# One fused graph, attention and expert layer: graph work placed earlier, two tiles turned later, expert choice from one partition

## The chip, the core and the metric

The kernel runs on one core of a Trainium2 chip. The metric is the device time of one execution in microseconds, the median of repeated runs on the chip. The core has TensorE (PE, with its weight loads PEld), VectorE (DVE), ScalarE (ACT), GpSimd (POOL) and SyncE (SP), which here only issues transfers. Each engine takes its instructions in order, so an instruction that waits holds all that stand behind it on that engine. The granted clock is the share of TensorE's full clock that the profiler records.

## The reference

The layer has 1250 tokens of width 768, all in float32. A graph with 21250 edges (`src`, `dst`) is fixed by the inputs. Cut to what matters:

```python
xn = layernorm(x)
# graph branch: two attention layers over the edges, with 4 and 2 heads
out1 = gat(layernorm(xn), edges, W1, 4 heads)
out2 = gat(out1, edges, W2, 2 heads)
graph = concat([xn, out2]) @ Wu + bu
# mixing branch: linear attention, then an MLP 768 -> 3072 -> 768
m = xn + linear_attention(layernorm(xn))
mix = m + gelu(layernorm(m) @ fc1 + fc1_b) @ fc2 + fc2_b
x = x + graph + mix
# experts: one choice of 2 of 4 for the whole sequence
v = layernorm(x)
logits = v.mean(tokens) @ router_w.T + router_b
e1, e2 = top2(logits);  g1, g2 = softmax of the two logits
out = x + layernorm(g1 * expert[e1](v) + g2 * expert[e2](v) + v)
```

An expert is 768 -> 1536 -> 768 with its own activation (gelu, silu or mish). Which expert's weights are needed is known only after the mean over all tokens.

## The kernel before

**Stages.** Tokens are held as 10 tiles of 125, or, turned, as `fT` (features on partitions). Matrices are multiplied with Strassen-like seven products: `differences` and `by_tokens` form the token-side differences in four VectorE operations per chunk of tokens, `combined` the weight-side ones. The stages follow each other: weight folding and the `Wu` product, the first graph product (`ps_g`), keys and values, queries and projection, the MLP with the graph attention woven into it, the choice of experts, then the two experts (`unit`, `second`) and the last tiles.

**Edges to a table.** The 21250 edges become a dense 1250 x 1250 table of counts in DRAM. `edge_piece` and `later_pieces` work through 10 pieces of 17 columns. For each piece a row of keys is broadcast to all partitions (`kr`, `load_keys`, 1062.5 KB), VectorE compares it with a column of keys and counts repeats (L295, L300, L305), and GpSimd issues 17 indirect transfers that add counts to one of two tables in turn (L315, 170 in all). `edge_piece(i)` of the first four pieces asks for the keys of piece i + 2 as soon as the buffer of piece i is free; before the change GpSimd's queue issues that load. When all 170 are done, `merged` adds the second table to the first by block of 125 rows (L1115), and `fetch` reads a block back (L1128).

**The graph in the MLP.** `gnn()` is a Python generator. Its first part, `largest`, finds the largest score per token: it issues three `merged`, then two `fetch`, yields, and then per block makes a mask `far` on VectorE (L1143) and updates a running maximum for each head (L1151 for the first block, L1147 for the others). Each `yield` carries a price in microseconds of TensorE time. The MLP loop pays with `spend`: 2.04 or 1.36 for one of the seven products of fc1, 1.39 for one half tile of fc2. The first call of `next(steps)` comes when the credit reaches zero:

```python
steps = gnn()
credit, cost = -44.0, 0.0
def spend(us):
    nonlocal credit, cost
    credit += 1.05 * us
    while cost is not None and credit >= cost:
        credit -= cost
        cost = next(steps, None)
```

The MLP takes 12 groups `g`, each with a chunk `c` of 4 token tiles and one of 6 (`MIX_TILES`); the patterns of `P` (an fc1 product) and `h` (a half tile of fc2, L1077, evicted by L1082 on VectorE) give the order of emission. `pin` keeps an instruction in order of the program among pinned ones of its engine; the framework's planner orders the rest by its own estimate of when operands are ready.

**The end of the MLP.** After the last half of a tile, `last_tile` calls `normal` (statistics, and the normalised tile `y`), and two tiles later `turned`: six matrix products against an identity with one more column of ones, which give `fT` and, in the last column, the sum over tokens (`pooled`). Of tile 9 the sum comes from seven other products (`ps_s9`, L1420 and L1425), so that it needn't wait for `y`.

**The choice.** `ps_g` (L1468) multiplies the sum with the router's weights, with the sum broadcast so that all 128 partitions get the 4 logits. `choose` finds the first expert in seven VectorE operations, and its number goes through a register of SyncE (`values_load`) into the address of the weights (`load_first`, L1545). Meanwhile TensorE turns tile 9 (L1479), then `warm(13)` multiplies identities.

**The experts.** For each pair `q` of hidden blocks and chunk `c`, `unit` makes seven products in two halves. `tables` has ScalarE work out four activation functions of the unit before, and `blended` mixes them on VectorE (L1530 to L1532).

Of the kernel before, what the change touches and what calls it, by code (L numbers as in the profile page):

```python
# [8 lines left out]
F32 = mybir.dt.float32  # L9
BF16 = mybir.dt.bfloat16  # L10
I32 = mybir.dt.int32
# [12 lines left out]
MIX, MIX_TILES = [(0, 250), (250, 375)], [(0, 1, 5, 6), (2, 3, 4, 7, 8, 9)]  # L24
# [8 lines left out]
def tile_gps_layer(ctx, tc, a, out):  # L33
    nc = tc.nc
# [66 lines left out]
    def differences(engine, of, to, c0, w):  # L101
        x11, x12, x21, x22 = (x[:, :, c0 : c0 + w] for x in of)
        t1, t2, t4 = (to[:, i, :, c0 : c0 + w] for i in range(3))
        for o, p, q in ((t1, x12, x11), (t2, x22, t1), (x12, x22, x12), (t4, x21, t2)):
            engine.tensor_tensor(o, p, q, ALU.subtract)

    def by_tokens(engine, to, c0, w):
        of = (fT[:, 0:3, :HALF], x12, fT[:, 3:6, :HALF], fT[:, 3:6, HALF:])
        differences(engine, of, to, c0, w)
# [212 lines left out]
    def edge_piece(i):  # L322
        kr = keys.pop(i)
        if i + 2 < SOON:
            load_keys(i + 2, nc.gpsimd)
        for _ in edge_steps(i, ep, kr, ((PIECE,),) * 3):
            pass
# [1036 lines left out]
    credit, cost = -44.0, 0.0  # L1364

    def spend(us):
        nonlocal credit, cost
        credit += 1.05 * us
        while cost is not None and credit >= cost:
            credit -= cost  # L1370
            cost = next(steps, None)

    ready = []

    def last_tile(t):
        normal(t)
        ready.append(t)
        if len(ready) > 2:
            turned(ready.pop(0))
# [14 lines left out]
    for g in range(GROUPS):  # L1394
# [4 lines left out]
        for c, pattern in enumerate(("PPhhhhPhhPPhhPPhhhh", "PPhhPhhPPhhPPhh")):  # L1399
            if g == GROUPS - 1 and c:  # L1400
# [3 lines left out]
                gnn_pool.__exit__(None, None, None)  # L1404
            parts = fc1_unit(g, c)
# [8 lines left out]
    for x in todo:  # L1414
        put_half(*x)
    turned(ready[0])

    t9 = NT - 1
    ps = bank("ps_s9")
    pin(nc.tensor.matmul(  # L1420
        ps[:, :KC], r3[:, t9, 1:2].to_broadcast([TP, 128]),
        identx[:, TP:].to_broadcast([TP, KC]), start=True, stop=False, skip_group_check=True,
# [42 lines left out]
    sels = const.tile([128, 2, 4], F32, name="sels")  # L1465
    ps = bank("ps_g")
# [8 lines left out]
    for j in range(2):  # L1475
        ps = bank4("ps_t")
        for i in range(3):
            k = 3 * j + i
            pin(nc.tensor.transpose(  # L1479
                ps[:, i, :TP], y[:, t9, k * 128 : (k + 1) * 128], ident[:TP, :TP]  # L1480
            ))
        nc.scalar.copy(fT[:, 3 * j : 3 * j + 3, t9 * TP :], ps[:, :3, :TP])
    warm(13)
    es = []

    def choose(j):
        l, m, first = lg[:, j, :], top[:, j, 0:1], top[:, j, 1:2]
        pin(nc.vector.tensor_reduce(m, l, AX.X, ALU.max))
        at = const.tile([128, 4], F32, name=f"at{j}")
        pin(nc.vector.scalar_tensor_tensor(at, l, m, order, op0=ALU.is_equal, op1=ALU.mult))  # L1490
        pin(nc.vector.tensor_reduce(first, at, AX.X, ALU.max))
        e_f = const.tile([128, 1], F32, name=f"e_f{j}")
        pin(nc.vector.tensor_scalar(e_f, first, -1.0, 4.0, op0=ALU.mult, op1=ALU.add))
        e_i = const.tile([128, 1], I32, name=f"e_i{j}")
        pin(nc.vector.tensor_scalar(e_i, e_f, 3.0, 0.0, op0=ALU.min, op1=ALU.max))
        pin(nc.vector.tensor_scalar(sels[:, j, :], at, first, None, op0=ALU.is_equal))
        if j == 0:
# [3 lines left out]
        es.append(nc.values_load(  # L1501
            e_i[0:1, 0:1], engines=[mybir.EngineType.SP], min_val=0, max_val=3,
            skip_runtime_bounds_check_because="clamped to 0..3 above",
        ))
# [159 lines left out]

    choose(0)
    load_first(0)
    by_tokens(vec, xt, *CHUNKS[0])
# [90 lines left out]
    for i in range(6):  # L1758
        for u in range(4):
# [11 lines left out]
            if i and u == 0:  # L1771

                for x in acts:
                    blended(*x)
# [12 lines left out]
            for x in acts:  # L1787
                blended(*x)
            acts = []
# [71 lines left out]
```

## Time and profile before

| what | us |
|---|---|
| median of three runs | 1904.69 (1903.83 to 1906.24) |
| the profiled execution, its own time | 1900.13 |
| its span, first to last instruction | 1898.2 |
| PE busy in the span | 1869.0 |
| DVE busy | 1336.0 |
| ACT busy | 803.3 |
| POOL busy | 498.0 |
| mean granted TensorE clock | 0.994 |

The profile is of one execution, the fastest of those shown by some microseconds; 1.9 us of its time lie outside its span. Busy times are sums over the span. A busy PE is not a PE at its peak, since the ends of matrix products are modelled. In rows of instructions, `x` is a count, and the bracket holds the engine's idle time before the row and what ended it. SPq and POOLq are the queues that issue transfers.

### The profile page before, as it was taken

How to read it: one execution, taken by the hardware profiler on the slowest of the kernel's cores; microseconds unless marked ns; L12 is line 12 of the kernel's file. 1: busy time of each engine (PE TensorE's matmuls, PEld its weight loads, DVE VectorE, ACT ScalarE, POOL GpSimd, SP SyncE). 2: the span in 40 equal slices, each digit the busy share in tenths (PEclk: the TensorE clock that was granted, in tenths of full speed). 3: DMA queues.
4: the chain of work that ended last, by engine and by line, in shares of the span. 5: the costliest groups of instructions: out<-in, count | busy, mean ns of one | idle time of the engine just before them, and what ended most of it. 6: DMA issues, size and time to landing. Idle time of an engine off the chain costs nothing.

```text
span 1898.2 us, 19544 instructions
## 1 busy us (share of the span) xinstructions
PE 1869.0 (98%) x6966; PEld 1245.7 (66%) x6966; DVE 1336.0 (70%) x2407; ACT 803.3 (42%) x1207; POOL 498.0 (26%) x341
## 2 busy tenths in 40 slices
PE   9999999999998999999999999999999999999998
PEld 7555556865565668787777655566766666666664
DVE  4656692677546967676666977766677777777778
ACT  3233221331321128777674186645364353433330
POOL 2265766687882110111111121000221000000000
PEclk9999999999998999999999999999999999999999
DMA  9748532523139751233343532202485201011023
GB/s 341 238 97 213 114 85 52 134 19 49 2 30 187 136 145 55 70 95 88 106 113 79 151 111 73 69 9 67 126 101 82 71 0 67 3 64 47 12 87 109
DMA packets 184285, 175.50 MB, mean 92 GB/s; under 512 B 110043, under 2 KB 153595, under 8 KB 182908
## 3 DMA queue, kind: packets, MB, share of 16 engines
q0 software_dynamic: 126640, 68.01, 20.8%
q1 hardware_dynamic: 54270, 98.48, 16.4%
q10 hardware_dynamic: 3278, 7.75, 1.3%
q8 instruction: 55, 0.90, 0.2%
q14 instruction: 42, 0.34, 0.1%
HBM read 137.80 MB, written 42.05 MB: 95 GB/s over the span
## 4 chain that ended last, share of the span: by engine, by line
PE 91%; DMA 4%; POOL 1%; DVE 1%; issue 1%; ACT 1%; SPq 0%; DVEq 0%; POOLq 0%; ACTq 0%
PE ps_f L1077 14%; PE ps_p L81 13%; PE ps_r L81 12%; PE ps_o L1255 7%; PE ps_a L127 7%; PE ps_g L578 4%; PE ps_u L545 4%; PE ps_p L974 4%; PE ps_c L127 3%; PE ps_f L1655 3%; PE ps_o L1294 2%; PE ps_va L127 2%; PE ps_ka L127 2%; PE ps_qa L127 2%; PE ps_d L127 2%; POOL tab L315 1%
## 5 line engine op out<-in xcount | busy, mean ns | idle before, releaser
L315 POOL DMA_INDIRECT tab<-mult,place_e x170 | 351.1, 2065 | 157.7 <-DMA tab<-mult,place_e 102.6
L1077 PE MATMUL ps_f<-w,v 128*125 128x384 f32 x960 | 338.9, 487 | 6.9 <-DVE slot_a L1082 6.9
L1077 PEld LDWEIGHTS ps_f<-w,v 128*125 128x125 f32 x960 | 178.0, 188 | 113.4 <-DVE slot_a L1082 8.0
L1082 DVE TENSOR_TENSOR slot_a<-ps_f,slot_a 125x384 f32<-125x384 f32 x240 | 131.6, 553 | 66.6 <-PE ps_f L1077 62.7
L1210 DVE TENSOR_TENSOR wt<-ee 125x375 f32<-125x375 f32 (+1 forms) x180 | 105.9, 590 | 84.5 <-PE ps_o L1255 57.5
L1255 PEld LDWEIGHTS ps_o<-turns,wt 125*125 125x125 f32 x800 | 137.1, 188 | 29.1 <-DVE wt L1211 4.0
L1255 PE MATMUL ps_o<-turns,wt 125*125 125x193 f32 x800 | 151.7, 329 | 2.9 <-DVE wt L1211 2.9
L1205 ACT ACTIVATE ee<-bt,s 125x375 f32<-125x375 f32 (+1 forms) x180 | 114.8, 638 | 77.1 <-DVE wt L1210 69.8
L81 PE MATMUL ps_p<-fT,w 128*128 128x312 f32 (+1 forms) x432 | 125.5, 426 | 0.6 <-ACT c L1573 0.6
L1211 DVE SCALAR_TENSOR_TENSOR wt<-wt,slot_x 125x375 f32<-125x375 f32 (+1 forms) x180 | 105.9, 590 | 4.4
L81 PEld LDWEIGHTS ps_p<-fT,w 128*128 128x128 f32 x432 | 81.5, 189 | 36.2 <-ACT c L1573 1.1
L81 PE MATMUL ps_r<-w,slot_a 128*125 128x384 f32 x260 | 94.5, 486 | 0.0
L127 PE MATMUL ps_a<-fT,w 128*128 128x250 f32 (+1 forms) x288 | 86.8, 432 | 0.7 <-DVE slot_a L979 0.7
L1617 DVE SCALAR_TENSOR_TENSOR slot_x<-ps_r,gate,slot_x 125x384 f32<-125x384 f32 x100 | 60.7, 615 | 33.3 <-PE ps_r L81 33.0
L81 PE MATMUL ps_p<-xt,ws 128*128 128x313 f32 (+1 forms) x288 | 83.6, 426 | 0.0
L578 PE MATMUL ps_g<-fx,zT 128*125 128x388 f32 x240 | 80.2, 490 | 1.5 <-DVE zT L372 1.5
L545 PE MATMUL ps_u<-wu,fT 128*125 128x384 f32 x240 | 79.9, 487 | 0.4 <-ACT fT L531 0.4
L974 PE MATMUL ps_p<-wp,slot_x 128*125 128x384 f32 x240 | 79.9, 486 | 0.0
L1147 DVE SCALAR_TENSOR_TENSOR slot_x<-turns,s,slot_x 125x1250 f32<-125x1250 f32 x54 | 79.4, 1512 | 0.1
L1026 ACT ACTIVATE v<-v,par 128x250 f32<-128x250 f32 (+1 forms) x72 | 40.0, 556 | 88.0 <-DVE v L1046 41.3
L1208 ACT ACTIVATE ee<-bt,s1l 125x375 f32<-125x375 f32 (+1 forms) x120 | 75.4, 628 | 0.1
L81 PE MATMUL ps_r<-w2s,ht 128*125 128x384 f32 x200 | 72.7, 486 | 0.0
(403 smaller groups left out, 3413.0 us busy)
## 6 DMA issues: line engine op xcount, KB each, us to landing
turns<-g_d POOLq DMA_DIRECT2D x12, 942.4 KB, 14.2
w<-in_L_mix_fc_w_dram SPq DMA_DIRECT2D x12, 768.0 KB
w<-in_L_mix_fc_w_dram SPq DMA_DIRECT2D x24, 384.0 KB
slot_x<-tab POOLq DMA_DIRECT2D x14, 610.4 KB, 6.6
w<-in_L_ffn_w_dram SPq DMA_DIRECT2D x11, 768.0 KB
w<-in_L_ffn_w_dram SPq DMA_DIRECT2D x5, 1536.0 KB
slot_x<-tab POOLq DMA_DIRECT2D x40, 183.1 KB, 3.3
kr_l<-key_d SPq DMA_DIRECT2D x6, 1062.5 KB
```

The source lines that it names most:

```text
L81: return lambda *args, **kw: pin(getattr(self.engine, name)(*args, **kw))
L127: engine.matmul(ps, wt[:, k, :], x[:, k, :], start=k == 0 and not more, stop=k == n - 1, skip_group_check=more,)
L315: nc.gpsimd.indirect_dma_start(out=tabs[c % 2][:, :], out_offset=bass.IndirectOffsetOnAxis(ap=place[:, c : c + 1], axis=0), in_=mult[:, c ...
L545: nc.tensor.matmul(ps[:TP, :w], fT[:, k, tc_], wu[:, k, c0 : c0 + w], start=k == 0, stop=k == KC - 1,)
L578: nc.tensor.matmul(ps[:TP, :388], zT[:, k, :], fx[:, k, h2 * 388 : (h2 + 1) * 388], start=k == 0, stop=k == KC - 1,)
L974: nc.tensor.matmul(ps[:TP, :w], qT[:, k, t * TP : (t + 1) * TP], pm[:, k, c0 : c0 + w], start=k == 0, stop=k == KC - 1,)
L1077: nc.tensor.matmul(ps, v_of[c][:, f, h, at : at + TP], lasts[g, j][:, f, :], start=f == 0, stop=f == 1,)
L1082: nc.vector.tensor_tensor(o, ps, o, ALU.add)
L1205: nc.scalar.activation(e[:, 0, :w], bt[:TP, 0, :w], AF.Exp, bias=s[:, 0, h, c : c + 1])
L1210: nc.vector.tensor_tensor(wt[:, :w], e[:, 0, :w], e[:, 1, :w], ALU.max)
L1211: nc.vector.scalar_tensor_tensor(wt[:, :w], wt[:, :w], 1.0, adj, op0=ALU.min, op1=ALU.mult)
L1255: nc.tensor.matmul(sums[i // 2][:TP, (i % 2) * 193 : (i % 2 + 1) * 193], wt[:, i * TP : (i + 1) * TP], gh[:, c, :], start=c == 0 and i % 2 ...
```

## The change

Four things are changed.

- The keys of pieces 2 and 3 are loaded by SyncE's queue in place of GpSimd's.
- The graph's generator starts with a credit of -20 in place of -44, and earns 1.01 in place of 1.05 per microsecond.
- The second chunk's tiles come in the order 2, 7, 3, 8, 4, 9. Tiles 3 and 8 are not turned in the MLP: GpSimd adds their `y`, six products with a column of ones put the sum into `ps_s9`, and they are turned together with tile 9 after the choice's products. The first expert's number comes from products for one partition (`ps_g1`), ahead of those for all partitions, and `warm(13)` becomes `warm(5)`. The first two of the four `by_tokens` operations come before the logits of all partitions are read.
- In the first group of expert units (`i == 0`), `blended` comes after the next unit's first evictions, no more at the end of its own unit.

```diff
--- before.py
+++ after.py
@@ -21,7 +21,7 @@
 HID = 1536
 FC = HID // 128
 HALF, CHUNKS = 625, [(0, 313), (313, 312)]
-MIX, MIX_TILES = [(0, 250), (250, 375)], [(0, 1, 5, 6), (2, 3, 4, 7, 8, 9)]
+MIX, MIX_TILES = [(0, 250), (250, 375)], [(0, 1, 5, 6), (2, 7, 3, 8, 4, 9)]
 GROUPS = 2 * HID // 256
 PAIRS = N * N
 PIECE, SOON = 17, 4
@@ -98,15 +98,15 @@
 
     x12 = fT[:, 0:3, HALF:]
 
-    def differences(engine, of, to, c0, w):
+    def differences(engine, of, to, c0, w, some=slice(0, 4)):
         x11, x12, x21, x22 = (x[:, :, c0 : c0 + w] for x in of)
         t1, t2, t4 = (to[:, i, :, c0 : c0 + w] for i in range(3))
-        for o, p, q in ((t1, x12, x11), (t2, x22, t1), (x12, x22, x12), (t4, x21, t2)):
+        for o, p, q in ((t1, x12, x11), (t2, x22, t1), (x12, x22, x12), (t4, x21, t2))[some]:
             engine.tensor_tensor(o, p, q, ALU.subtract)
 
-    def by_tokens(engine, to, c0, w):
+    def by_tokens(engine, to, c0, w, some=slice(0, 4)):
         of = (fT[:, 0:3, :HALF], x12, fT[:, 3:6, :HALF], fT[:, 3:6, HALF:])
-        differences(engine, of, to, c0, w)
+        differences(engine, of, to, c0, w, some)
 
     def combined(engine, w11, w12, w21, w22, to):
 
@@ -322,7 +322,7 @@
     def edge_piece(i):
         kr = keys.pop(i)
         if i + 2 < SOON:
-            load_keys(i + 2, nc.gpsimd)
+            load_keys(i + 2, nc.sync)
         for _ in edge_steps(i, ep, kr, ((PIECE,),) * 3):
             pass
 
@@ -1361,22 +1361,37 @@
 
 
     steps = gnn()
-    credit, cost = -44.0, 0.0
+    credit, cost = -20.0, 0.0
 
     def spend(us):
         nonlocal credit, cost
-        credit += 1.05 * us
+        credit += 1.01 * us
         while cost is not None and credit >= cost:
             credit -= cost
             cost = next(steps, None)
 
     ready = []
 
+
+
+    deferred = MIX_TILES[1][2:4]
+    of_them = []
+
     def last_tile(t):
         normal(t)
-        ready.append(t)
-        if len(ready) > 2:
-            turned(ready.pop(0))
+        if t in deferred:
+            if t == deferred[0]:
+                of_them.append(y[:, t, :])
+            else:
+                total = later.tile([TP, D], F32, name="total") if t == deferred[1] else of_them[0]
+                nc.gpsimd.tensor_tensor(total, of_them[0], y[:, t, :], ALU.add)
+                of_them[0] = total
+            if ready:
+                turned(ready.pop(0))
+        elif t < NT - 1:
+            ready.append(t)
+            if len(ready) > 2:
+                turned(ready.pop(0))
 
     def halves_of(g, c):
         ts = MIX_TILES[c]
@@ -1402,6 +1417,7 @@
                     pass
                 cost = None
                 gnn_pool.__exit__(None, None, None)
+                later = mlps.enter_context(tc.tile_pool(name="later", bufs=1))
             parts = fc1_unit(g, c)
             for p in pattern:
                 if p == "P":
@@ -1413,13 +1429,20 @@
             todo = halves_of(g, c)
     for x in todo:
         put_half(*x)
-    turned(ready[0])
+    for t in ready:
+        turned(t)
 
     t9 = NT - 1
     ps = bank("ps_s9")
+    ones_k = identx[:, TP:]
+    for k in range(KC):
+        pin(nc.tensor.matmul(
+            ps[:, k : k + 1], of_them[0][:, k * 128 : (k + 1) * 128], ones_k,
+            start=k == 0, stop=False, skip_group_check=True,
+        ))
     pin(nc.tensor.matmul(
-        ps[:, :KC], r3[:, t9, 1:2].to_broadcast([TP, 128]),
-        identx[:, TP:].to_broadcast([TP, KC]), start=True, stop=False, skip_group_check=True,
+        ps[:, :KC], r3[:, t9, 1:2].to_broadcast([TP, 128]), ones_k.to_broadcast([TP, KC]),
+        start=False, stop=False, skip_group_check=True,
     ))
     for k in range(KC):
         pin(nc.tensor.matmul(
@@ -1463,6 +1486,38 @@
     lg = const.tile([128, 2, 4], F32, name="lg")
     top = const.tile([128, 2, 2], F32, name="top")
     sels = const.tile([128, 2, 4], F32, name="sels")
+
+    es, number = [], const.tile([1, 4], F32, name="number")
+    ps = bank("ps_g1")
+    for k in range(KC):
+        pin(nc.tensor.matmul(
+            ps[:1, :4], pooled[:, k : k + 1], rw[:, k, :], start=k == 0, stop=k == KC - 1
+        ))
+    pin(nc.vector.scalar_tensor_tensor(
+        number, ps[:1, :4], 1.0 / N, rb[:1], op0=ALU.mult, op1=ALU.add
+    ))
+
+    def first_of(l, m, first, at, n):
+        pin(nc.vector.tensor_reduce(m, l, AX.X, ALU.max))
+        pin(nc.vector.scalar_tensor_tensor(
+            at, l, m, order[:n], op0=ALU.is_equal, op1=ALU.mult
+        ))
+        pin(nc.vector.tensor_reduce(first, at, AX.X, ALU.max))
+
+    def load_number(first, j):
+        e_f = const.tile([128, 1], F32, name=f"e_f{j}")
+        pin(nc.vector.tensor_scalar(e_f[:1], first, -1.0, 4.0, op0=ALU.mult, op1=ALU.add))
+        e_i = const.tile([128, 1], I32, name=f"e_i{j}")
+        pin(nc.vector.tensor_scalar(e_i[:1], e_f[:1], 3.0, 0.0, op0=ALU.min, op1=ALU.max))
+        es.append(nc.values_load(
+            e_i[0:1, 0:1], engines=[mybir.EngineType.SP], min_val=0, max_val=3,
+            skip_runtime_bounds_check_because="clamped to 0..3 above",
+        ))
+
+    top0, at0 = const.tile([1, 2], F32, name="top0"), const.tile([1, 4], F32, name="at0_")
+    first_of(number, top0[:, 0:1], top0[:, 1:2], at0, 1)
+    load_number(top0[:, 1:2], 0)
+    by_tokens(vec, xt, *CHUNKS[0], slice(0, 2))
     ps = bank("ps_g")
     for k in range(KC):
         pin(nc.tensor.matmul(
@@ -1472,36 +1527,30 @@
     pin(nc.vector.scalar_tensor_tensor(
         lg[:, 0, :], ps[:, :4], 1.0 / N, rb, op0=ALU.mult, op1=ALU.add
     ))
-    for j in range(2):
-        ps = bank4("ps_t")
-        for i in range(3):
-            k = 3 * j + i
-            pin(nc.tensor.transpose(
-                ps[:, i, :TP], y[:, t9, k * 128 : (k + 1) * 128], ident[:TP, :TP]
-            ))
-        nc.scalar.copy(fT[:, 3 * j : 3 * j + 3, t9 * TP :], ps[:, :3, :TP])
-    warm(13)
-    es = []
+    for t in (*deferred, t9):
+        for j in range(2):
+            ps = bank4("ps_t")
+            for i in range(3):
+                k = 3 * j + i
+                pin(nc.tensor.transpose(
+                    ps[:, i, :TP], y[:, t, k * 128 : (k + 1) * 128], ident[:TP, :TP]
+                ))
+            nc.scalar.copy(
+                fT[:, 3 * j : 3 * j + 3, t * TP : (t + 1) * TP], ps[:, :3, :TP]
+            )
+    warm(5)
 
     def choose(j):
         l, m, first = lg[:, j, :], top[:, j, 0:1], top[:, j, 1:2]
-        pin(nc.vector.tensor_reduce(m, l, AX.X, ALU.max))
         at = const.tile([128, 4], F32, name=f"at{j}")
-        pin(nc.vector.scalar_tensor_tensor(at, l, m, order, op0=ALU.is_equal, op1=ALU.mult))
-        pin(nc.vector.tensor_reduce(first, at, AX.X, ALU.max))
-        e_f = const.tile([128, 1], F32, name=f"e_f{j}")
-        pin(nc.vector.tensor_scalar(e_f, first, -1.0, 4.0, op0=ALU.mult, op1=ALU.add))
-        e_i = const.tile([128, 1], I32, name=f"e_i{j}")
-        pin(nc.vector.tensor_scalar(e_i, e_f, 3.0, 0.0, op0=ALU.min, op1=ALU.max))
+        first_of(l, m, first, at, 128)
         pin(nc.vector.tensor_scalar(sels[:, j, :], at, first, None, op0=ALU.is_equal))
         if j == 0:
             pin(nc.vector.scalar_tensor_tensor(
                 lg[:, 1, :], sels[:, 0, :], NEG, l, op0=ALU.mult, op1=ALU.add
             ))
-        es.append(nc.values_load(
-            e_i[0:1, 0:1], engines=[mybir.EngineType.SP], min_val=0, max_val=3,
-            skip_runtime_bounds_check_because="clamped to 0..3 above",
-        ))
+        else:
+            load_number(first[:1], 1)
 
     slots = [{}, {}]
 
@@ -1662,9 +1711,9 @@
                 )
             yield t
 
+    load_first(0)
     choose(0)
-    load_first(0)
-    by_tokens(vec, xt, *CHUNKS[0])
+    by_tokens(vec, xt, *CHUNKS[0], slice(2, 4))
     choose(1)
     load_second(0, second_buffer())
     for j in range(2):
@@ -1768,10 +1817,9 @@
             if i and u:
                 two = rest.pop(0)
                 next(two)
-            if i and u == 0:
-
-                for x in acts:
-                    blended(*x)
+
+            for x in acts:
+                blended(*x)
             if i == 0 and u == 1:
                 gates()
             if i == 0 and u == 2:
@@ -1784,9 +1832,10 @@
             next(steps)
             if i and u:
                 next(two)
-            for x in acts:
-                blended(*x)
-            acts = []
+            if i:
+                for x in acts:
+                    blended(*x)
+                acts = []
             held = [(slots[i // 3], 2 * q, *CHUNKS[c], i == 0 and c == 0)]
             if i and u == 0:
                 if i > 1:
```

## The prediction

> **What bounds the kernel now.** I read the page first, then the stages one by one (the table of windows), then TensorE's waits, and last the order of time around each wait.
>
> ```profile
> PE 1869.0 (98%) x6966; PEld 1245.7 (66%) x6966; DVE 1336.0 (70%) x2407; ACT 803.3 (42%) x1207; POOL 498.0 (26%) x341
> ...
> 520.00:600.00 80.00, 72.47 (x251) 47.11 (x250) 34.33 (x59) 14.87 (x30) 48.57 (x29) 0.95 0.66 87
> ...
> 1330.00:1346.00 16.00, 15.10 (x91) 13.80 (x90) 9.84 (x31) 4.24 (x10) 0.00 (x0) 0.79 0.37 117
> 1346.00:1400.00 54.00, 51.04 (x193) 36.13 (x194) 43.11 (x76) 30.30 (x31) 19.43 (x8) 1.00 0.71 119
> ...
> PE ps_f L1077 <- DVE slot_a L1082: 6.9, 1, 6.9
> PE ps_p L81 <- DVE c L1579: 3.0, 2, 1.8
> ```
>
> TensorE is busy for 1869.0 of 1898.2 us, so only work on it and its waits count. The columns of a window are its length, then PE, PEld, DVE, ACT and POOL, clock, DMA share and GB/s. TensorE loses 7.5 us in 520 to 600 and 3 us in 1346 to 1400; the waits name the causes, an eviction on VectorE each time. The change touches both places, and the choice of experts between them.
>
> The long wait comes about so (order of time):
>
> ```profile
> 558.94 0.56 DVE L1082 TENSOR_TENSOR slot_a<-ps_f,slot_a 125x384 f32<-125x384 f32 x1 [0.80 <-PE ps_f L1077]
> ...
> 562.61 1.43 PE L127 MATMUL ps_a<-xt,ws 128*128 128x250 f32 x6
> ...
> 564.44 4.63 POOL L1115 DMA_DIRECT2D tab<-tab  x3 [2.14 <-DMA tab<-mult,place_e]
> ...
> 576.00 0.57 POOL L1128 DMA_DIRECT2D slot_x<-tab  x1 [6.93 <-PE ps_f L1077]
> ...
> 590.54 0.96 DVE L1143 TENSOR_SCALAR turns<-slot_x 125x1250 f32<-125x1250 f32 x1 [10.53 <-DMA slot_x<-tab]
> 591.54 1.74 DVE L1151 TENSOR_SCALAR slot_x<-turns,s 125x1250 f32<-125x1250 f32 x2
> ...
> 595.83 2.92 PE L1077 MATMUL ps_f<-w,v 128*125 128x384 f32 x4 [6.86 <-DVE slot_a L1082]
> ```
>
> GpSimd ends its 170 indirect transfers at 562.3, merges three blocks and fetches one; it reaches VectorE at 590.5. VectorE stood at the first mask (L1143) from 580.0, with the evictions L1082 behind it. TensorE ran on for 8.9 us on its banks, then stopped for 6.86. So the graph already begins too early for its data.
>
> **Earlier graph: the main term.** When does VectorE meet the first mask? It is emitted when the credit has paid the start and the first yield of 9. Before: (44 + 9) / 1.05 = 50.5 us of MLP. The first group's second chunk pays 7 x 2.04 + 8 x 1.39 = 25.4; the next chunk pays 7 x 1.36 + 12 x 1.39 = 26.2, to 51.6. So the mask falls behind the last half tile of that chunk, the L1082 that ran at 579.46: that is where the trace has it. The planner kept the order of emission there. After: (20 + 9) / 1.01 = 28.7. At 25.4 two products bring 28.1 and the first half tile 29.5, so the mask comes right after the eviction at 558.94, ending 559.5. From there TensorE can fill the three banks of `ps_f` and make one fc1 product, to 563.9; then its next half tile needs an eviction. The mask and two L1151 end 2.7 us after the data come, at 593.2, and an eviction of 0.56 later TensorE runs again at 593.9. The stall is 30.0 us, 23.1 more than now, if the data come when they do now. TensorE has no idle time from 600 to 1330 beyond some 4 us, so nothing later gives this back. The end of the graph doesn't move: it costs 1.05 x 553 - 44 = 537 of credit by the MLP work done when it ends at 1264 (my count), and (537 + 20) / 1.01 = 551, the same place.
>
> **What makes the data earlier.** The keys of pieces 2 and 3 leave GpSimd's queue.
>
> ```profile
> 100.49 1.40 POOL L276 DMA_DIRECT2D kr<-key_d  x1
> ...
> 107.05 2.37 DVE L295 TENSOR_TENSOR eq<-kr,kcol 125x2125 bf16<-125x2125 f32 x1 [6.50 <-DMA kr<-key_d]
> ...
> 560.30 2.00 POOL L315 DMA_INDIRECT tab<-mult,place_e  x1 [0.30 <-issue]
> ```
>
> The two issues take 0.53 and 1.40 us of GpSimd. The page "DMA: Bandwidth & Descriptors" of the Trainium skill (Issuing engines are not separate DMA queues) says that transfers from any engine share the same 16 DMA engines, and that another issuer saves only the sequencer's time. By this rule the chain ends 1.9 us sooner, against the earlier start's 22. The trace allows more: the first indirect transfer, issued at 57.18 behind the keys of piece 2 in one queue, needs 13.3 us to land, where 3.7 is the median, and the next waits for it. Without those keys ahead it may win 2 to 8, but the DMA engines are at a share of 1.0 until 72, and the second takes 11.4 with no keys ahead. On SyncE the keys stand behind loads that it issues until 83.8, and then meet the third to fifth indirect transfers, so I give part back. I take 3 us, bounds 0 and 8; late in the chain each issue starts 2.3 after the last, so a gain made early is kept. VectorE's wait of 6.5 goes, but one of about 2 for piece 2's keys comes; TensorE waited for neither. On SyncE behind the keys stands the `wk` load, not issued before 116, so I cost that queue at nothing; were the keys ahead of the `x` loads at 49 to 59, these would be held until the compare ends at 52, a bound of 3 us. A stopped MLP asks for its next weights (issued at 566.6) later, and the merges run in less traffic: 2 us, bounds 0 and 4. The term is 23.1 - 3 - 2 = +18.
>
> **Choice of experts.** TensorE is in one chain from tile 2's halves at 1308.24 to the first expert product (chain of waits):
>
> ```profile
> 1333.74 1.35 PE ps_s L1425 x12
> ...
> 1335.33 2.72 PE ps_g L1468 x12
> 1338.06 1.35 PE ps_t L1479 x6
> 1339.41 4.29 PE ps_warm L81 x26
> 1343.70 1.60 PE ps_p L81 x6
> ```
>
> Per tile 2.58 for two halves and 1.34 for a turned one. Before: 6 x 3.92 + 1.60 + 1.47 + 0.24 + 2.72 + 1.35 + 4.29 = 35.2, in the trace 35.5. After: six tiles' halves and four turned, 20.8; six products with ones, as L1425, 1.35; tile 4 turned, 1.60; that is 1332.0. Tile 9's statistics, three VectorE rounds of about 3.5 us behind tile 8's, come at 1332.5 (1332.9 now): they set `ps_s9`, done at 1334.0, `pooled` 0.24 later. Then `ps_g1`: as many products as `ps_g` with one column of weights, so between 0.7 and 2.72, taken 1.36; `ps_g` 2.72; three tiles turned 4.05; five warm 1.65: first expert product at 1344.0, against 1343.70. The number is ready 2.5 us sooner (SyncE's load at 1337.8 against 1340.31), but TensorE isn't free for the weights. I take +0.3, bounds -1.5 and +1.7. GpSimd's addition of 125 x 768 has no row; VectorE's of 128 x 768 takes 0.95; tile 8's `y` comes about 1326, so even 5 us are covered, and uncovered it would hold `ps_s9`. VectorE has some 1 us more of small operations, behind which the weight sums still start before 1345.68.
>
> A rule that speaks against fewer warm products: the page "TensorE: Matmul & The Clock Gate" (Part 1) has the clock fall to half after a window of about 3.4 us without enough work, and come back after one as long of steady work. The windows show 0.50 from 1336 to 1342 and 0.95 after, so 4.0 us of turning and warming from 1338.06. Five warm ones alone (1.65) would leave about 2 us at half speed, a loss of 1; with twelve more transposes the stretch is 5.7, and I take 0.
>
> **Blending.** The 3.0 us of waits for L1579 come from three `blended` operations of 1.5 us that stand ahead of the next unit's evictions. After the change those evictions come first. Gain 3.0, less 0.5 for the blend that now meets `by_hidden` in the next group; bounds -3 and +1. I take -2.5.
>
> **Sum.** 18 + 0.3 - 2.5 = +15.8 on the profiled 1900.13, that is 1915.9. This execution lies 4.56 under the median of the runs shown, so I add the sum to the median: 1904.69 + 15.8 = 1920.5.
>
> **Rivals.**
> 1. *The likeliest, 0.72*: as above. With its bounds the graph term lies at 10 to 24, the time at 1912 to 1928.
> 2. *The edges end much sooner, or the planner puts the mask later, 0.20.* If the serial first six indirect transfers (57 to 102) shrink to their bare landing of 3.9 each, GpSimd gains 20 us and the stall is near today's. Or the planner, which orders by its own estimate, delays the mask: then the start doesn't do what it says. Against it: the second mask too stands where emission has it. At best the wait of 6.86 goes as well: -2 to -9, so 1896 to 1903. It decides from a gain of about 19 us at the mask.
> 3. *About equal, 0.08*: half of that gain in DMA and less stall; the terms cancel within 4 us.
> The gain of the choice alone, up to 1.5, cannot turn the sign.
>
> **Numbers.** A difference of 0.2% (3.8 us) is about what a measurement of this kernel can tell from none. Faster 0.20, same 0.08, slower 0.72. The likeliest case alone gives 1912 to 1928; to hold 8 in 10 the range reaches to 1899.
>
> **What would show it.** Right: the 170th indirect transfer ends within 8 us of 562; the first mask's idle time is about 28 us or more, and TensorE's wait for `slot_a` near 25 to 30 us around 564 to 592; no wait for L1579 in the first expert units; the first expert product some 35 us after tile 2's halves. Wrong: the last indirect transfer near 540, or a first mask behind later evictions than the first half tile of that chunk, with a stall no longer than 10 us.

## The result, and the profile after

After the change the median is 1925.69 us (1915.48 to 1929.39, 6 runs), against 1904.26 (1900.89 to 1907.02, 6 runs) of the kernel before beside it: 21.4 us slower in the medians. The ratio on record, taken from all the runs, is 1.0106, with a 95% interval of 1.0082 to 1.0129. The profiled execution of after took 1927.76 us; its span is 27.7 us longer than that of before, because this one lies 2.1 us above its median and that one 4.1 below.

First the page of after and its table of windows, then the waits of TensorE (total, times, longest):

```profile
PE 1867.6 (97%) x6962; PEld 1243.9 (65%) x6962; DVE 1338.8 (70%) x2407; ACT 806.9 (42%) x1209; POOL 499.6 (26%) x340
...
520.00:600.00 80.00, 44.36 (x161) 29.14 (x160) 19.04 (x37) 12.04 (x24) 55.00 (x31) 0.79 0.52 55
1356.00:1372.00 16.00, 15.19 (x91) 13.29 (x91) 10.73 (x37) 4.93 (x10) 0.00 (x0) 0.68 0.55 189
...
PE ps_f L1077 <- DVE slot_a L1082: 35.5, 1, 35.5
PE ps_p L81 <- ACT c L1622: 3.2, 2, 2.7
PE ps_t L1350 <- ACT slot_x L1342: 1.3, 1, 1.3
PE ps_p L81 <- DVE c L1628: 0.8, 1, 0.8
```

TensorE has about the same work as before, but in 520 to 600 it is busy for 44.36 us where it was 72.47. The wait for the half tile's eviction grew from 6.9 to 35.5 us. The wait for `c` on ScalarE (L1622 here is L1573 of before) grew from 0.6 to 3.2 us, that for `c` on VectorE (L1628, before L1579) fell from 3.0 to 0.8, and one for tile 4's `y` (L1342) is new. I cut both profiles at the same instructions:

| stretch | before | after | difference |
|---|---|---|---|
| start to the MLP's first half tile (L1077) | 530.6 | 531.6 | +1.0 |
| from there to tile 2's halves in the last group | 777.7 | 801.1 | +23.4 |
| from there to the first expert product | 35.3 | 36.4 | +1.1 |
| the expert units, to the first product of the last tiles | 495.2 | 497.5 | +2.3 |
| the rest | 59.5 | 59.4 | -0.1 |

The long wait in after, in order of time (the bracket is the engine's idle time and what ended it):

```profile
559.92 0.56 DVE L1082 TENSOR_TENSOR slot_a<-ps_f,slot_a 125x384 f32<-125x384 f32 x1 [0.80 <-PE ps_f L1077]
...
563.59 1.43 PE L127 MATMUL ps_a<-xt,ws 128*128 128x250 f32 x6
574.60 4.59 POOL L1115 DMA_DIRECT2D tab<-tab  x3 [2.13 <-DMA tab<-mult,place_e]
585.63 0.58 POOL L1128 DMA_DIRECT2D slot_x<-tab  x1 [6.44 <-issue]
...
599.19 0.81 DVE L1143 TENSOR_SCALAR turns<-slot_x 125x1250 f32<-125x1250 f32 x1 [38.72 <-DMA slot_x<-tab]
599.92 0.55 DVE L1082 TENSOR_TENSOR slot_a<-ps_f,slot_a 125x384 f32<-125x384 f32 x1
600.39 1.64 DVE L1151 TENSOR_SCALAR slot_x<-turns,s 125x1250 f32<-125x1250 f32 x2
...
600.53 2.92 PE L1077 MATMUL ps_f<-w,v 128*125 128x384 f32 x4 [35.51 <-DVE slot_a L1082]
```

VectorE stands at the first mask from the end of the eviction at 559.92, and the next eviction, which comes behind the mask in its order, runs at 599.92; TensorE runs on to 565 and stops. GpSimd's merges start at 574.60, 10 us later than before, so the mask's block comes at 599.2 where it came at 590.5. One detail differs from my forecast: the next eviction follows right behind the first mask, ahead of the two L1151.

### The profile page after: what moved, and what is told of

Same layout as the page of the kernel before. It is cut to its first block, busy times and chain, and to the rows that moved or that the text cites. A ratio compares the mean times of both kernels' runs of the same rounds, so it can differ in the third digit from the quotient of the medians.

```text
span 1925.9 us, 19540 instructions
## 1 busy us (share of the span) xinstructions
PE 1867.6 (97%) x6962; PEld 1243.9 (65%) x6962; DVE 1338.8 (70%) x2407; ACT 806.9 (42%) x1209; POOL 499.6 (26%) x340
## 3 DMA queue, kind: packets, MB, share of 16 engines
q0 software_dynamic: 126352, 65.84, 20.5%
## 4 chain that ended last, share of the span: by engine, by line
PE 86%; POOL 4%; issue 4%; DVE 3%; DMA 2%; ACT 1%; ACTq 0%; SPq 0%; DVEq 0%; POOLq 0%
PE ps_f L1077 15%; PE ps_p L81 13%; PE ps_r L81 11%; PE ps_a L127 7%; PE ps_o L1255 7%; PE ps_u L545 4%; POOL tab L315 4%; PE ps_g L578 4%; PE ps_c L127 3%; PE ps_f L1704 3%; PE ps_o L1294 2%; PE ps_va L127 2%; PE ps_ka L127 2%; PE ps_qa L127 2%; PE ps_d L127 2%
## 5 line engine op out<-in xcount | busy, mean ns | idle before, releaser
L1077 PE MATMUL ps_f<-w,v 128*125 128x384 f32 x960 | 339.5, 488 | 35.5 <-DVE slot_a L1082 35.5
L1077 PEld LDWEIGHTS ps_f<-w,v 128*125 128x125 f32 x960 | 178.3, 188 | 142.1 <-DVE slot_a L1082 36.6
L1255 PEld LDWEIGHTS ps_o<-turns,wt 125*125 125x125 f32 x800 | 136.0, 187 | 26.2 <-issue 0.7
L1255 PE MATMUL ps_o<-turns,wt 125*125 125x193 f32 x800 | 149.7, 327 | 0.0
L1026 ACT ACTIVATE v<-v,par 128x250 f32<-128x250 f32 (+1 forms) x72 | 40.0, 555 | 73.2 <-DVE v L1066 28.3
```

What stands on the lines that cost most here:

```text
L1077: nc.tensor.matmul(ps, v_of[c][:, f, h, at : at + TP], lasts[g, j][:, f, :], start=f == 0, stop=f == 1,)
L1255: nc.tensor.matmul(sums[i // 2][:TP, (i % 2) * 193 : (i % 2 + 1) * 193], wt[:, i * TP : (i + 1) * TP], gh[:, c, :], start=c == 0 and i % 2 ...
```

## The experiments

Each is timed against the kernel before on the same chip; its median moved between 1898.7 and 1905.0 from one set of runs to the next, so only the ratios are compared. "Last issue" is the start of the last indirect transfer of the edge chain in the profile.

### The four parts, each alone

**The start alone** (start_only).

```diff
-    credit, cost = -44.0, 0.0
+    credit, cost = -20.0, 0.0
-        credit += 1.05 * us
+        credit += 1.01 * us
```

> The kernel before with only the graph's start moved (credit -20, rate 1.01). Theory: the start is nearly the whole change. The first mask sits behind the first half tile, TensorE's wait for slot_a is about 30 us (35.5 in the changed kernel, where the indirect transfers ended 10 us later), and the time is 1904 + 20 to 25. Rival, that the keys on SyncE make the indirect transfers late: with the keys still on GpSimd the 170th issue stands near 560 and the time is at most 1904 + 20, with the rest, about 8, showing when the keys alone are moved. Rival, that the planner's other choices matter: less than +10.

Measured: ratio 1.0057 (1.0037 to 1.0077), or +10.9 us (7.0 to 14.7), where I expected 20 to 25. The long wait comes back without the rest of the change, and in the profile the stretch of the MLP takes 798.2 us, 20.5 more than in before. The profile shows more than the medians because this execution lies 5.0 us above its own median, and that of before 4.1 below.

```profile
596.55 0.99 DVE L1143 TENSOR_SCALAR turns<-slot_x 125x1250 f32<-125x1250 f32 x1 [36.06 <-DMA slot_x<-tab]
598.06 4.90 PE L1077 MATMUL ps_f<-w,v 128*125 128x384 f32 x8 [33.03 <-DVE slot_a L1082]
```

**The blending alone** (blend_only). Before with the two places of `blended` as in after.

```diff
-            if i and u == 0:
-
-                for x in acts:
-                    blended(*x)
+
+            for x in acts:
+                blended(*x)
...
-            for x in acts:
-                blended(*x)
-            acts = []
+            if i:
+                for x in acts:
+                    blended(*x)
+                acts = []
```

> The kernel before with only the blending moved in the first group of expert units. Theory: ScalarE's tables now wait for the later blending, its copy of the first product stands behind them, and TensorE waits for that copy some 2.7 us and falls to half clock for 5: from the first expert product to the first product of the last tiles 497.4 us against 495.2, so +2. Rival, that this wait belongs to the other parts (earlier weights, half clock at the start of the units): the waits for L1579 vanish and nothing takes their place, -2.5.

Measured: ratio 1.0014 (0.9997 to 1.003); the median does not tell this from no change. The expert units do: they take 497.6 us in its profile, and 497.4 to 497.6 in all four profiles with the later blend, against 495.2 to 495.5 in the nine with the old one. Why is seen in after, ScalarE's rows first, then TensorE's:

```profile
1403.72 1.25 ACT L1571 ACTIVATE th<-slot_a 128x1248 f32<-128x1248 f32 x1 [6.70 <-DVE slot_a L1581]
...
1411.81 0.40 ACT L1622 COPY c<-ps_p 128x312 f32<-128x312 f32 x1
...
1412.26 2.19 PE L81 MATMUL ps_p<-fT,w 128*128 128x312 f32 x6 [2.65 <-ACT c L1622]
1414.24 3.12 PE L81 MATMUL ps_p<-xt,w 128*128 128x312 f32 x6
```

ScalarE's functions for the next unit write into `th` and `gl`, of which there is one buffer each, and the last operation of `blended` (L1581) still reads them. With the blend later, ScalarE sits idle for 6.70 us before them, and its copy of `p1` for the running unit stands behind all of them in its queue. TensorE adds its next product to `p1`, so it waits for that copy: 2.65 us, and then two products at 2.19 and 3.12 us where a product takes 1.74.

In this run the data happen to reach the mask at the same time as in the start alone, which makes them a pair:

```profile
596.59 0.98 DVE L1143 TENSOR_SCALAR turns<-slot_x 125x1250 f32<-125x1250 f32 x1 [15.04 <-DMA slot_x<-tab]
601.79 2.92 PE L1077 MATMUL ps_f<-w,v 128*125 128x384 f32 x4 [11.30 <-DVE slot_a L1082]
```

With equal data, the earlier start makes TensorE wait 33.03 us instead of 11.30: +21.7. The stretch of the MLP grows by less, 798.2 against 780.6, +17.6, since a wait of 3.5 us for the graph's attention weights `wt` near 720 (L1255) is gone with the earlier start.

**The keys alone** (keys_only).

```diff
-            load_keys(i + 2, nc.gpsimd)
+            load_keys(i + 2, nc.sync)
```

> The kernel before with only the keys of pieces 2 and 3 on SyncE. Theory: the indirect transfers keep their own pace, their end varies by some us from run to run, and the time is within 4 us of 1904. Rival, that the keys on SyncE collide with the third to fifth indirect transfers: the 170th issue starts near 570 in place of 560, VectorE's wait at the first mask is about 20 us in place of 10.5, TensorE's about 17 in place of 6.9, the time 1904 + 10. Rival, that leaving GpSimd's queue helps: issue near 557, time 1904 - 3.

Measured: ratio 1.0021 (1.0003 to 1.0038). Slower, where I had 3 us of gain. In its profile the last issue is at 565.20, the mask's idle time 17.15 us and the wait for `slot_a` 13.51, on the side of the rival that expected a collision, though below its 570, 20 and 17. GpSimd's rows, then SyncE's issue of the keys:

```profile
57.51 2.13 POOL L315 DMA_INDIRECT tab<-mult,place_e  x1 [35.26 <-DVE place_e L313]
71.12 2.01 POOL L315 DMA_INDIRECT tab<-mult,place_e  x1 [11.49 <-DMA tab<-mult,place_e]
85.93 1.99 POOL L315 DMA_INDIRECT tab<-mult,place_e  x1 [12.80 <-DMA tab<-mult,place_e]
96.48 2.43 POOL L315 DMA_INDIRECT tab<-mult,place_e  x1 [8.56 <-DMA tab<-mult,place_e]
...
L276 SPq DMA_DIRECT2D kr<-key_d x2: 1706/1850/1993, 73.2 to 75.3; - x2
```

Nothing of piece 2's keys stands ahead of the first transfer any more, and it still holds the second back to 71.12 (71.38 before). It lands after 13.3 us in both: the keys were not what made it slow. Both loads are issued at 73.2 and 75.3, into the second and third transfers; the third now starts 2.8 us later than before and the fourth 6.9. But this delay is made up on the way. Below are the starts of some transfers of the chain in us, and the rows of the 102nd, in before and then in keys_only:

| transfer | before | keys_only | key3_only |
|---|---|---|---|
| 4th | 89.6 | 96.5 | 93.9 |
| 13th | 118.5 | 125.8 | 118.7 |
| 18th | 137.3 | 138.0 | 135.1 |
| 102nd | 397.5 | 397.1 | 395.3 |
| 170th, the last | 560.3 | 565.2 | 558.7 |

```profile
397.51 2.00 POOL L315 DMA_INDIRECT tab<-mult,place_e  x1 [0.30 <-issue]
397.09 2.04 POOL L315 DMA_INDIRECT tab<-mult,place_e  x1 [0.30 <-issue]
```

By the 102nd transfer keys_only is level with before, so its late end came about behind that, where the chain no longer shows the early delay. The collision with the keys is shown; that it made the run slower is not.

**Keys of piece 3 alone** (key3_only: `load_keys(i + 2, nc.sync if i else nc.gpsimd)`).

> Before with the keys of piece 3 alone over SyncE; piece 2's stay on GpSimd's queue ahead of the first indirect transfer. If the transfers of the two pieces' keys meeting the third to fifth indirect transfer is what delays the chain: piece 3's keys start at 74 to 76, the second to fifth indirect transfer are late by about half as much as in keys_only (the fourth issued at 92 to 94 where before has 90 and keys_only 96.6), and the thirteenth is at 119 to 123 (before 118.5, keys_only 125.9); ratio 1.000 to 1.002. If the delay came from somewhere else than these transfers: the thirteenth at 118.5 or sooner, since GpSimd is spared the 1.4 us issue at 100.49.

Measured: ratio 0.9974 (0.995 to 0.9998), faster, which neither side expected. The fourth transfer starts at 93.88, between the 89.6 of before and the 96.5 of keys_only, as one load instead of two should give. But by the thirteenth the delay is gone (118.66, before 118.47), sooner than I expected:

```profile
93.88 1.99 POOL L315 DMA_INDIRECT tab<-mult,place_e  x1 [6.95 <-DMA tab<-mult,place_e]
```

Before has a wait of 1.1 us and an issue of 3.65 us at 107.63, behind GpSimd's own issue of these keys at 100.49; here there is neither. So both loads together delay the thirteenth transfer, and piece 3's alone does not. How much of either median comes from the keys is not settled: over all profiles the fifteenth transfer starts at 127.4 to 129.7 with piece 2's and 3's keys on GpSimd and at 130.0 to 130.6 with both on SyncE, 1 to 2 us apart, while the last issue is spread much wider, 557.0 to 566.0 (seven kernels) against 560.7 to 571.1 (four), by what happens in between. In after and rest_only the 35th transfer starts at 199.5, and at 188.2 to 195.7 in the other twelve; keys_only and after_later load the same keys over SyncE and are not among the late ones, so that this isn't traced to the keys either.

**The choice alone** (choice_only): the part from `deferred` to `warm(5)`, with all else as before.

> The kernel before with only the choice of experts changed: order of tiles, tiles 3 and 8 turned later, first number from one partition, five warm products, the differences split. Theory: from tile 2's halves to the first expert product 36.4 us as in the changed kernel, against 35.3, so +1. Rival, that the half clock there (0.50 to 1369 in the changed kernel) came from the state left by the long stall: 35.3 or less, and -1.

Measured: ratio 1.0003 (0.9986 to 1.0021). From tile 2's halves to the first expert product it takes 34.90 us, not the 36.4 that I expected, and 1.27 of them are a wait that before has not. The clock makes the rest: choice_only and after_later (35.11) have half clock for 6.8 us of this stretch, as before has with its 35.29; after and rest_only have it for 10.2 and take 36.4 each. What brings the longer half clock is not settled: it stands behind stalls of 35.5 and 15.9 us in the MLP, the shorter one behind stalls of 10.0 us and less, and no run changes the one without the other. In after the same place reads:

```profile
1354.94 1.60 PE L1350 MATMUL ps_t<-identx,slot_x 125*128 125x126 f32 x12 [1.27 <-ACT slot_x L1342]
1356.38 1.40 PE L1439 MATMUL ps_s<-identx,total 125*128 125x1 f32 x12
...
1359.79 0.44 PE L1493 MATMUL ps_g<-rw,pooled 128*1 128x4 f32 x12 [0.26 <-DVE pooled L1452]
1360.16 2.72 PE L1523 MATMUL ps_g<-rw,pooled 128*128 128x4 f32 x12
1362.74 4.39 PE L1535 MATMUL ps_t<-ident,slot_x 125*128 125x125 f32 x18
1366.93 2.34 PE L81 MATMUL ps_warm<-ident 128*128 128x128 f32 x10
1369.07 1.84 PE L81 MATMUL ps_p<-fT,w 128*128 128x313 f32 x6
```

TensorE comes to turn tile 4 right after tile 9's halves, and ScalarE has not yet written tile 4's `y`. Before the change another tile was turned in between, which covered this.

**Tile 4 after the products with ones** (choice_swap: the choice alone, with one move):

```diff
-    for t in ready:
-        turned(t)
     ps = bank("ps_s9")
     ones_k = identx[:, TP:]
     for k in range(KC):
         pin(nc.tensor.matmul(...ones_k...))
+    for t in ready:
+        turned(t)
```

> choice_only with tile 4 turned after the six products with ones instead of ahead of them. Theory (the choice lost 1.27 us because tile 4 is turned before ScalarE has written its y): no wait over 0.3 at L1350, the number's products (ps_g1) 1.0 to 1.3 us sooner after tile 2's halves than in choice_only (26.93 there), tile 2's halves to the first expert product 33.4 to 33.9. Rival (tile 9's statistics on VectorE are as late as that wait): the wait moves to ps_s, gain under 0.4 us.

Measured, one execution: the wait is gone, and with it 1.34 us up to the number's products (25.59 us after tile 2's halves, 26.93 in the choice alone); the first expert product comes after 33.83.

```profile
1323.62 1.40 PE L1436 MATMUL ps_s<-identx,total 125*128 125x1 f32 x12
1325.06 1.60 PE L1350 MATMUL ps_t<-identx,slot_x 125*128 125x126 f32 x12
```

### All but the start, and the start the other way

**After without its start** (rest_only: -44 and 1.05 put back).

> After with the graph's start and rate put back (-44, 1.05): keys over SyncE, choice and blending as in after. If the parts add: keys +4.0, choice +0.7, blending +2.6 from their single runs, so +7 us, ratio 1.003 to 1.005; the start's share of the whole is then after less this, +11 to +14 in the medians. If the parts work on each other (late keys cost more with an early start than with the old one): this run at +1 to +4 and after less this at 17 or more. The mask's idle time 13 to 20, the wait for slot_a 10 to 17.

Measured: ratio 1.0029 (1.0007 to 1.0051), the mask's idle time 19.84 us and the wait for `slot_a` 15.93, units 497.4. The parts add up: 0.57% + 0.21% + 0.03% + 0.14% is 0.95%, the whole is 1.06%, and the start's share of the whole, 1.06% - 0.29% = 0.77% or 14.7 us, lies at the upper end of what it costs alone.

**Before with a later start** (later_start).

```diff
-    credit, cost = -44.0, 0.0
+    credit, cost = -60.0, 0.0
-        credit += 1.05 * us
+        credit += 1.084 * us
```

> Before with the graph's credit begun at -60 and paid at 1.084 (the opposite direction of the change; end of the graph at the same place: (537 + 60) / 1.084 = 551). The first mask is emitted after (60 + 9) / 1.084 = 63.7 us of MLP in place of 50.5, some 13 us later. My theory (stall = time at which the data come, less the time at which VectorE meets the mask, less about 9 us that TensorE runs on): the mask's idle time is 0 to 3 us when the last indirect transfer is issued near 560 and up to 8 when near 566, and TensorE has no wait for slot_a over 1 us. It gains the 7 to 11 us of that wait less a wait for ps_o that grows by 0 to 4: -3 to -8 on the median, ratio 0.996 to 0.9985, with less spread than before. Rival (the graph's work that is put later comes back as waits behind it, at ps_o or in the drain before the last group): 0 or slower, ratio 0.9995 to 1.002.

Measured: 1892.76 us (1890.89 to 1896.14), ratio 0.9973 (0.9956 to 0.999): faster than both kernels. VectorE comes to the mask when the data are there, with no idle time:

```profile
591.33 0.80 DVE L1143 TENSOR_SCALAR turns<-slot_x 125x1250 f32<-125x1250 f32 x1
```

Before ran from 1890.52 to 1908.37 beside it. The lower ends agree; what the later start cuts off is the upper part of the range. That these are the executions in which the edge chain ended late fits the account, but the one profile is of the fastest execution, with the last issue at 558.70, and shows no late chain.

**After with the later start** (after_later: -60 and 1.084 instead of -20 and 1.01).

> After with the start of later_start (-60, 1.084); keys over SyncE, choice and blending as in after. The data come at 597 to 600, VectorE meets the mask at 591, TensorE's banks cover 9 us: the mask's idle time 5 to 9, the wait for slot_a 0 to 1. Theory (late keys cost only through this mask, choice and blending cost what the single runs show): later_start's 0.9973 plus 1.3 to 2.7 us of the choice and 2.3 of the blending, ratio 0.999 to 1.000; tile 2's halves to the first expert product 34.9 to 36.5, units 497.4. If late keys or the combination cost elsewhere too: 1.002 or more.

Measured: ratio 0.9988 (0.9969 to 1.0007). Its MLP stretch takes 769.25 us, that of later_start 769.28, and the 2.9 us between the two spans are the choice (+1.3: 35.11 against 33.84, with 6.8 us of half clock against 3.4) and the units (+2.0: 497.35 against 495.39). The two ratios differ by 0.15%, also 2.9 us, so that these two leave nothing for the keys over SyncE once the mask comes later. The mask's idle time was 1.04 us where I had 5 to 9, because the last issue came at 560.65 this time.

### The data's side: a shorter chain

If the stall is only the data's lateness, then it must vanish with earlier data as well. Two kernels, before_short with the old start and start_short with the early one, leave out the last piece's 17 indirect transfers, so that their table lacks those edges:

```diff
-        for c in range(c0, c0 + PIECE):
+        for c in range(c0, c0 + PIECE * (i + 1 < EC // PIECE)):
             nc.gpsimd.indirect_dma_start(
```

> Before with the last piece's 17 indirect transfers left out (the table lacks those edges); all else, start and rate included, as before. The last of 153 is issued near 522, its blocks come some 30 us later, at 552, while VectorE meets the first mask at 580. Theory (the stall is only data later than the mask): no idle time at the mask, no wait for slot_a, ratio 0.994 to 0.998.

> start_only with the last piece's 17 indirect transfers left out, as in before_short. VectorE meets the first mask right after the first half tile's eviction, near 560, the blocks are there from 552. Theory: the wait for slot_a of 33.0 us goes to 0, and with it the whole loss of the early start: ratio to before 0.992 to 0.998, within 3 us of before_short. Rival (an early start costs by itself: masks and products of the graph stand before evictions from the first chunk on, whenever the data come): waits of some us stay at L1082 and other lines and start_short is 5 us or more above before_short.

Measured: ratio 0.9965 (0.995 to 0.9981) with the old start, 0.9937 (0.9917 to 0.9957) with the early one. With the last issue at 520.8, the early start's mask has no wait at all (start_short):

```profile
559.27 0.56 DVE L1082 TENSOR_TENSOR slot_a<-ps_f,slot_a 125x384 f32<-125x384 f32 x1 [0.80 <-PE ps_f L1077]
559.75 0.80 DVE L1143 TENSOR_SCALAR turns<-slot_x 125x1250 f32<-125x1250 f32 x1
560.57 0.56 DVE L1082 TENSOR_TENSOR slot_a<-ps_f,slot_a 125x384 f32<-125x384 f32 x1
```

The early start is then the better one, by 5.5 us in the medians (1885.58 against 1891.09), more than I had allowed: it spares the wait at L1255 (3.45 us in before_short) and 3.4 us of half clock behind it. The start is thus not bad by itself. It is bad for data that come near 590.

### The copy on VectorE

**The blending alone, with the copy of `p1` moved for two pairs** (blend_copy).

```diff
-        pin(nc.scalar.copy(c1, p1))
+        (vec if q in (1, 2) else act).__getattr__('tensor_copy' if q in (1, 2) else 'copy')(c1, p1)
```

> blend_only with one thing more: the copy c1 of the first expert units of q = 1 and 2 goes to VectorE instead of ScalarE, where it stands behind the tables that wait for the later blend. My theory (what turned the gain of the blend into a loss is ScalarE's order): TensorE's wait of 2.65 us for c L1573 is gone, with it the products at half clock behind it, and the units take 493 to 495 us (blend_only 497.6, before 495.2); ratio to before 0.998 to 1.000. Rival (VectorE is the bound there: the blend moved behind the evictions is late whoever copies): a wait for VectorE takes its place, units 496 or more, ratio 1.001 or more.

Measured: ratio 0.999 (0.9968 to 1.0013). The wait for ScalarE's copy is gone and the units come down from 497.6 to 495.5, so ScalarE's order was the cause. But they are not better than before (495.2): VectorE now makes TensorE wait 1.38 us for the weight sums that stand behind the blend, and 1.85 for the moved copy itself a unit later, which stands behind the next blend.

```profile
PE ps_p L81 <- DVE c L81: 1.8, 1, 1.8
PE ps_p L81 <- DVE ws L81: 1.4, 1, 1.4
```

Both ends of the rivals were half right: the cause was ScalarE, and with it cured VectorE takes its place.

## Why the prediction was right, and where its steps were off

The sign and the main mechanism held. I had forecast +15.8 us and 1920.5; measured were +21.4 and 1925.69. Two of the four steps had the wrong sign, and part of the nearness is luck. By its own steps:

1. **Earlier graph, the main term.** Right in place: the mask stands right after the first half tile's eviction (559.92), with 38.7 us of idle time, and TensorE stops from 565 to 600.5. Shown by later_start (no stall), by start_short (no stall with earlier data) and by the pair at equal data. The +23.1 was mis-sized: the pair gives +21.7. I had the next eviction behind the two L1151; it came right after the first mask, so that TensorE restarts 1.5 us after the mask begins, and I had 3.4. What I said of "nothing later gives this back" was wrong: the early start spares the wait at L1255 (2.9 us in before, 3.5 in the pair) and the slower clock behind it, so that the MLP's stretch grew by 17.6. In the medians the start costs 10.9 us alone and 14.7 as the whole less rest_only. (The bounds of 10 to 24 that I gave this term are, from its own parts, 11 to 23.)
2. **What makes the data earlier.** The step that failed. I took 3 us from the keys, with bounds of 0 and 8; keys_only lost 4.0 (0.2% of 1905, interval 0.6 to 7.2). My argument was that the first transfer was slow because of the keys ahead of it. It was as slow without them. I had named the collision with the third to fifth transfers and taken it for a part of a gain; it was all that the start of the chain shows, 6.9 us later at the fourth transfer and 7.3 at the thirteenth. By the 102nd this is gone too, so that the cause of the 4.0 us stays open. The rule that I quoted from the Trainium skill ("DMA: Bandwidth & Descriptors", Issuing engines are not separate DMA queues), that another issuer shares the same 16 DMA engines and saves only sequencer time, allowed 1.9 us of gain, and stood nearer to the result than my reading of the trace. The 2 us for less traffic are not seen: from the last issue to the mask it takes 28.7 us in after and 30.5 in start_only, and 28.6 to 33.2 in the kernels with the old start in which the mask waited.
3. **Choice of experts.** I took +0.3; the profile of after has +1.1, which comes with 10.2 us of half clock in place of 6.8, and the choice alone is unresolved in its median (-2.7 to +4.0 us). Three terms were off. Tile 4's turning waits 1.27 us for its `y`, which I had not costed. `ps_g1` takes 0.44 us, below my lower bound of 0.7. The five warm products took 2.34 in after, at half clock, and 1.28 in the choice alone; I took 1.65, and set the clock's loss at 0 against the 1 us that I had worked out from the rule of the Trainium skill ("TensorE: Matmul & The Clock Gate", Part 1) for a short stretch. Both happen.
4. **Blending.** I took -2.5 with bounds of -3 and +1; it was +2.3. The waits for L1579 fell from 3.0 to 0.8, but I followed only VectorE's queue. ScalarE's tables wait for the buffers that the blend reads, and ScalarE's copy, which TensorE needs, stands behind the tables. blend_copy showed that this is the cause.

Against the pair at equal data: 17.6 for the start, 4.0 for the keys, 1.1 and 2.3 are 25.0, somewhat above the 21.4 of the medians. That difference is within the intervals of the terms. The forecast of the sum came this near because errors of opposite sign met: the stall of +23.1 was 5.5 too large against the 17.6 of the pair, while the 3, 2 and 2.5 us that I took off for the keys, the traffic and the blending did not come.

## What to carry to other kernels

When work that waits for data is emitted into an in-order queue ahead of evictions, cost it from the time its data come: emit it no sooner than that less what TensorE can still do with its free result banks (8.9 us in before), and at a late rather than an early moment if the data's time varies. When one operation is moved on an engine, follow the second engine that reads its buffer, and what stands behind it there. Moving a transfer to another queue also moves it in time; look at what it then meets, and whether a delay is still there where the data are used.

## What the runs showed of the hardware

- **One program's indirect chain does not take one time.** The last of 170 transfers was issued between 557.0 and 566.0 us in seven kernels with the same edge code and queues. It goes into the stall: in the eight profiles with the old start in which the mask waited, TensorE's wait for `slot_a` mostly grows with it, from 0.95 us (557.0) over 6.86 (560.3) to 13.51 (565.2) and 15.93 (571.1, with the keys on SyncE). With the mask late it hardly does: later_start ranges over 5 us in 12 runs, before beside it over 18 in 35.
- **A wait of TensorE mostly cost more than its length.** Windows of before around its two waits in the MLP (TensorE's busy time second, the granted clock third from the end):

```profile
596.00:598.00 2.00, 2.00 (x4) 1.07 (x5) 1.97 (x3) 0.00 (x0) 0.93 (x2) 0.50 1.28 155
600.00:602.00 2.00, 2.00 (x5) 1.09 (x5) 2.00 (x3) 0.00 (x0) 0.00 (x0) 0.63 1.03 225
...
714.00:716.00 2.00, 1.75 (x5) 1.75 (x6) 1.97 (x5) 1.96 (x4) 0.00 (x0) 0.53 0.00 0
```

  The clock is at half for 5.7 us after the wait of 6.86, and for 3.3 after that of 2.91. From the MLP on, the 14 profiles have 24 waits of TensorE of 2.65 us or more. Behind 23 of them TensorE worked for 3.0 to 5.9 us at half clock, whether the wait was 3 us long or 35; half of that, 1.5 to 2.9 us, is my estimate of what each cost. Behind one it did not, 3.51 us long in choice_only and ended at 718.2:

```profile
718.00:720.00 2.00, 1.83 (x10) 1.70 (x11) 1.97 (x5) 1.97 (x3) 0.00 (x0) 1.00 0.00 0
```

  The MLP's stretch less all its waits fits this: 761.5 us in start_short, which has no such wait there, 763.9 to 765.5 in the six with one, 764.2 (choice_only) to 767.5 in the seven with two.
- **The same instructions, two times.** Among the kernels with the old choice, tile 2's halves to the first expert product take 33.6 to 33.8 us in five and 35.3 in four. In the four, 6.8 us of them are at half clock, `ps_g` among them (2.72 us in before); in the five 3.4 or none, and `ps_g` runs at full in key3_only (1.50). That fits what the Trainium skill says ("TensorE: Matmul & The Clock Gate", Part 1), that the clock's window runs free of the kernel; no run here sets its phase, so this cause is not shown. A difference of 1.6 us there says nothing about a change.
